# Layer 1's edge groups: two VectorE inputs placed in PSUM, the running sums scaled on ScalarE, three banks of node sums

## The chip, the cores and the metric

The kernel runs on one core of a Trainium2 chip. The metric is device time in microseconds (us), from three runs of which the median is taken. One further execution was recorded by the hardware profiler; all durations of single instructions come from that one.

## The reference, cut to what matters

A graph of 3125 nodes and 50000 edges, sorted by target, goes through two layers, each with a message-passing part, an attention-like part and a feed-forward part. The change touches the message-passing part of layer 1 alone:

```python
h_fwd = h @ W_forward.T                     # 3125 x 64
h_rev = h @ W_reverse.T
messages = h_fwd[src] * direction[:, 0:1] + h_rev[src] * direction[:, 1:2]
scores = leaky_relu(messages @ attn.T, 0.2)             # 4 heads
exp_scores = exp(scores - scores.max(axis=0))
sum_exp = segment_sum(exp_scores, dst)
norm = exp_scores / (sum_exp[dst] + 1e-10)
out = [segment_sum(messages * norm[:, h:h+1], dst) for h in range(4)]
```

For each edge a row is fetched from a table by the edge's source, combined into a message of 64 numbers and four scores, weighted by four exponentials, and summed into the edge's target node.

## The kernel before

The stages run one after the other: layer 0's mixing and feed-forward, then layer 1's sorting, mixing and feed-forward. `layer1_mix` first writes a table `tab1` of 3125 rows (forward and reverse message and scores side by side, 2 x 68 numbers). It then goes over the edges in 391 columns of 128, taken in 49 groups of 8 (`GROUP`). Node sums are kept in SBUF as `acc`, 25 tiles of 125 nodes by 4 heads by 65 numbers (64 of the message and the weight itself).

A group passes through these functions:

- `fetch`: eight indirect DMAs issued by GpSimd (L51), one for each column of 128 edges, into the tile `g1` (four buffers). They are asked for three groups ahead.
- `messages` (L1223 to L1234): VectorE combines the two halves of the fetched rows, forms the scores and their maximum over the group, and TensorE transposes the maximum.
- `maximum` (L1241 to L1247): VectorE updates the running maximum `top`, TensorE spreads it to all partitions.
- `ones_of` (L1272): for each node tile that the group's edges can reach, VectorE builds a 0/1 matrix `hot` from the edges' targets `t_dst` and the row of numbers `node`. Both inputs lie in SBUF. There are 99 of these in all, about two a group.
- `exponents` (L1252 to L1257): VectorE subtracts the maximum, ScalarE writes the exponentials into the 65th column of `v1`, and `grown`, the factor by which older sums must shrink.
- `weigh` (L1280): VectorE multiplies the messages by each head's exponential, 2048 results a partition. Both inputs lie in SBUF, the second being that 65th column.
- `products` (L1288): TensorE multiplies `hot` by `v1` into a PSUM bank `pw`, one for each node tile (four banks). One product in the code is two records in the trace.
- `add` (L1297, L1299): for a node tile that already has sums, VectorE multiplies `acc` by `grown` and then adds `pw`; a new tile is copied by ScalarE (L1302).

The loop is a software pipeline: turn i holds `messages(i)`, `weigh(i-1)`, `maximum(i)`, `products(i-1)`, `add(i-2)`, `ones_of(i)` and `exponents(i)`. TensorE, VectorE and ScalarE keep the order in which the code calls them (`manual_schedule`); GpSimd's queue holds the gathers. Twice a turn `next(todo)` puts in a piece of `galerkin`, layer 1's other part: in the first 26 turns or so two 512-wide TensorE products with their ScalarE copies and square (L1551 to L1559), VectorE's L1547 to L1563 and TensorE's L1565; later one small piece every other turn (L1602).

Of the kernel before, what the change touches and what calls it, by code (L numbers as in the profile page):

```python
# [8 lines left out]
F32 = mybir.dt.float32  # L9
I32 = mybir.dt.int32  # L10
BF16 = mybir.dt.bfloat16
AF = mybir.ActivationFunctionType
OP = mybir.AluOpType
AX = mybir.AxisListType
PSUM = bass.MemoryType.PSUM
# [4 lines left out]
P = 125  # L20
# [5 lines left out]
GROUP = 8  # L26
# [62 lines left out]
class Kernel:  # L89
# [1082 lines left out]
    def layer1_mix(self):  # L1172
        nc, tc, a = self.nc, self.tc, self.a
        W, HD = 68, 64
        with ExitStack() as m:
# [11 lines left out]
            gp = m.enter_context(tc.tile_pool(name="l1g", bufs=3))  # L1187
            ps_a = m.enter_context(tc.tile_pool(name="l1pa", bufs=2, space=PSUM))
            ps_c = m.enter_context(tc.tile_pool(name="l1pc", bufs=1, space=PSUM))
            ps_w = m.enter_context(tc.tile_pool(name="l1pw", bufs=4, space=PSUM))  # L1190
            ps_s = m.enter_context(tc.tile_pool(name="l1ps", bufs=1, space=PSUM))


# [7 lines left out]
            acc = big.tile([P, NT, 4, HD + 1], F32, name="acc1")  # L1201
# [4 lines left out]
            def tiles_of(j):  # L1206

                return max(0, (128 * j - DRIFT) // 2000), min(NT - 1, (128 * j + 127 + DRIFT) // 2000)

            begun = set()  # L1210

            def fetch(j0):
                n = min(GROUP, NJ - j0)
                g = gp.tile([128, GROUP, 2 * W], F32, name="g1", bufs=4)
                for i in range(n):
                    gather(nc, g[:, i, :], tab1[:], self.t_src[:, j0 + i:j0 + i + 1])
                return j0, n, g

            def messages(j0, n, g):

                d = self.t_dir[:, j0:j0 + n, :]
                o = gp.tile([128, GROUP, W], F32, name="msg1")
                nc.vector.tensor_mul(o[:, :n, :], g[:, :n, :W], d[:, :, 0:1].to_broadcast([128, n, W]))  # L1223
                nc.vector.tensor_mul(g[:, :n, W:], g[:, :n, W:], d[:, :, 1:2].to_broadcast([128, n, W]))
                nc.vector.tensor_add(o[:, :n, :], o[:, :n, :], g[:, :n, W:])
                s = gp.tile([128, GROUP, 4], F32, name="score1")
                nc.vector.scalar_tensor_tensor(s[:, :n, :], o[:, :n, HD:], 0.2, o[:, :n, HD:],
                                               op0=OP.mult, op1=OP.max)
                if j0 + n == NJ:
                    nc.vector.tensor_scalar(s[:, n - 1, :], s[:, n - 1, :], late, None, op0=OP.add)  # L1230
                mx = gp.tile([128, 4], F32, name="mx1")
                nc.vector.tensor_reduce(mx, s[:, :n, :].rearrange("p j h -> p h j"), AX.X, OP.max)
                pt = ps_s.tile([4, 128], F32, name="psm")
                nc.tensor.transpose(pt, mx, self.ident)  # L1234
                return o, s, pt

            def maximum(pt):

                nonlocal top
                two = gp.tile([4, 3], F32, name="top")  # L1240
                nc.vector.tensor_reduce(two[:, 2:3], pt, AX.X, OP.max)  # L1241
                nc.vector.tensor_tensor(two[:, 0:1], two[:, 2:3], top, OP.max)
                nc.vector.tensor_sub(two[:, 1:2], top, two[:, 0:1])
                top = two[:, 0:1]
                pb = ps_s.tile([128, 2, 4], F32, name="psm")
                for i in range(2):
                    nc.tensor.transpose(pb[:, i, :], two[:, i:i + 1].to_broadcast([4, 128]), self.ident[:4, :4])  # L1247
                return pb

            def exponents(n, s, pb):  # L1250
                big2 = gp.tile([128, 2, 4], F32, name="top_b", bufs=4)
                nc.vector.tensor_copy(big2, pb)  # L1252
                nc.vector.tensor_sub(s[:, :n, :], s[:, :n, :], big2[:, 0:1, :].to_broadcast([128, n, 4]))
                v = gp.tile([128, GROUP, 4, HD + 1], F32, name="v1", bufs=2)
                nc.scalar.activation(v[:, :n, :, HD], s[:, :n, :], AF.Exp)
                grown = gp.tile([128, 4], F32, name="grown", bufs=4)
                nc.scalar.activation(grown, big2[:, 1, :], AF.Exp)  # L1257
                return big2, grown, v

            def tiles_in(j0, n):  # L1260

                w0, w1 = tiles_of(j0)[0], tiles_of(j0 + n - 1)[1]
                for w in range(w0, w1 + 1):
                    js = [i for i in range(n) if tiles_of(j0 + i)[0] <= w <= tiles_of(j0 + i)[1]]
                    yield w, js[0], len(js)

            def ones_of(j0, n):

                hots = []
                for w, i0, k in tiles_in(j0, n):  # L1270
                    hot = gp.tile([128, GROUP, P], F32, name="hot", bufs=5)
                    nc.vector.scalar_tensor_tensor(  # L1272
                        hot[:, :k, :], self.t_dst[:, j0 + i0:j0 + i0 + k, None].to_broadcast([128, k, P]),
                        float(-w * P), self.node[:, None, :P].to_broadcast([128, k, P]),
                        op0=OP.add, op1=OP.is_equal)
                    hots.append(hot)
                return hots

            def weigh(n, o, v):
                nc.vector.tensor_mul(v[:, :n, :, :HD], o[:, :n, None, :HD].to_broadcast([128, n, 4, HD]),  # L1280
                                     v[:, :n, :, HD:].to_broadcast([128, n, 4, HD]))

            def products(j0, n, v, hots):
                sums = []
                for (w, i0, k), hot in zip(tiles_in(j0, n), hots):
                    pw = ps_w.tile([P, 4, HD + 1], F32, name="pw")
                    for i in range(i0, i0 + k):
                        nc.tensor.matmul(pw.rearrange("p h c -> p (h c)"), hot[:, i - i0, :],  # L1288
                                         v[:, i, :, :].rearrange("p h c -> p (h c)"),
                                         start=(i == i0), stop=(i == i0 + k - 1))  # L1290
                    sums.append(pw)
                return sums

            def add(j0, n, big2, grown, sums):
                for (w, _, _), pw in zip(tiles_in(j0, n), sums):
                    if w in begun:
                        nc.vector.tensor_mul(acc[:, w, :, :], acc[:, w, :, :],  # L1297
                                             grown[:P, :, None].to_broadcast([P, 4, HD + 1]))
                        nc.vector.tensor_add(acc[:, w, :, :], acc[:, w, :, :], pw)  # L1299
                    else:  # L1300
                        begun.add(w)
                        nc.scalar.copy(acc[:, w, :, :], pw)  # L1302
                    if j0 + n == NJ or w < tiles_of(j0 + n)[0]:
                        nc.scalar.copy(unit[:, w, :], big2[:P, 0, :])


            with tc.manual_schedule(engines={E_.PE, E_.DVE, E_.Activation}):
                todo = self.galerkin(big, wk, ps_a, ps_c, xT)
                next(todo)
                starts = [(j0, min(GROUP, NJ - j0)) for j0 in range(0, NJ, GROUP)]  # L1310
                G = len(starts)
                ahead = [fetch(starts[i][0]) for i in range(3)]
                msg, exps, summed = {}, {}, {}
                for i in range(G + 2):
                    if i + 3 < G:
                        ahead.append(fetch(starts[i + 3][0]))
                    if i < G:
                        j0, n, g = ahead[i]
                        o, s, pt = messages(j0, n, g)
                    next(todo, None)  # L1320
                    if 0 <= i - 1 < G:
                        weigh(starts[i - 1][1], msg[i - 1][0], exps[i - 1][2])
                    if i < G:
                        pb = maximum(pt)
                    if 0 <= i - 1 < G:
                        summed[i - 1] = products(*starts[i - 1], exps[i - 1][2], msg[i - 1][1])
                    if 0 <= i - 2 < G:
                        add(*starts[i - 2], *exps[i - 2][:2], summed[i - 2])
                    if i < G:
                        msg[i] = o, ones_of(j0, n)  # L1330
                        exps[i] = exponents(n, s, pb)
                    next(todo, None)
                last = exps[G - 1][0]
# [14 lines left out]
            for t0, n in CHUNKS:  # L1348
                s = slice(t0, t0 + n)
# [649 lines left out]
```

## Time and profile before

| what | value |
|---|---|
| median of three runs | 3148.76 us (3139.96 to 3158.86) |
| profiled execution, its own time | 2766.24 us |
| profiled execution, span | 2764.5 us |
| gathers of this stage, first start to last end | 1612.2 to 2190.7 us after the span's start |
| 391 gathers: busy, mean | 459.6 us, 1175 ns |
| groups 3 to 25 (start of L1223 to that of group 26) | 1665.2 to 1938.6 us |
| groups 26 to 47 | 1938.6 to 2192.8 us |

The profiled execution is 382 us shorter than the median of the runs shown. The page gives no reason for it. "Busy" is an engine's own work; "idle before" is the time that it stood still ahead of an instruction, with what ended it. A line number such as L51 can be that of a helper, so that gathers of several stages share it; they are told apart by their tiles (`g<-tab,t_src` here).

### The profile page before, as it was taken

Reading aid. Unit: us, or ns where it says so; the run is one execution under the profiler, and the core shown is the slowest. Engines: PE = TensorE matmul, PEld = TensorE weight load, DVE = VectorE, ACT = ScalarE, POOL = GpSimd, SP = SyncE. Lnnn points to the kernel's source line nnn. Section 1 sums busy time; section 2 is a strip of 40 time slices with the busy share of each in tenths; the row PEclk is TensorE's granted clock in tenths of the full one; section 3 lists DMA queues with packets and bytes.
Section 4 is the critical chain, followed back from the end, with each engine's and each line's share of the span. In section 5 each row is a group of like instructions: output and inputs, shape, how many; then the busy total and the mean of one; then the engine's idle time right before and its main releaser. Section 6 shows DMA issues by size and latency. Waiting matters only on the chain. (4 is left out here: it accounts for less than half of the span.)

```text
span 2764.5 us, 26618 instructions
## 1 busy us (share of the span) xinstructions
PE 2192.9 (79%) x9047; PEld 1649.0 (60%) x9047; DVE 1502.0 (54%) x3575; ACT 545.3 (20%) x1115; POOL 1660.4 (60%) x1486
## 2 busy tenths in 40 slices
PE   1762659999976997899999459998777756999953
PEld 1541447866754665788888336665655544666643
DVE  7986499455477901122112449998777760222226
ACT  2420000000011111222222234444000021223313
POOL 4888787774000813666666158778777507777751
PEclk9955669999986999999999669999898868999976
DMA  8930534133400303455554421111111121112252
GB/s 296 382 111 14 118 76 107 43 72 91 115 32 2 87 19 130 157 179 180 191 196 139 113 76 47 48 48 45 47 48 49 37 68 39 26 40 60 54 105 71
DMA packets 175937, 259.79 MB, mean 94 GB/s; under 512 B 53839, under 2 KB 140857, under 8 KB 172402
## 3 DMA queue, kind: packets, MB, share of 16 engines
q1 hardware_dynamic: 114273, 198.43, 23.2%
q0 software_dynamic: 52288, 47.17, 7.3%
q10 hardware_dynamic: 9222, 12.30, 1.5%
q8 instruction: 76, 1.25, 0.2%
q14 instruction: 78, 0.64, 0.1%
HBM read 173.99 MB, written 83.69 MB: 93 GB/s over the span
## 5 line engine op out<-in xcount | busy, mean ns | idle before, releaser
L58 POOL DMA_INDIRECT adj<-ch_sum,ch_place x391 | 506.3, 1295 | 150.4 <-issue 111.6
L51 POOL DMA_INDIRECT g<-tab,t_src x391 | 459.6, 1175 | 119.7 <-issue 106.8
L58 POOL DMA_INDIRECT sorted<-s_rows,pos x256 | 245.1, 958 | 183.5 <-DVE s_rows L1059 114.0
L460 PE MATMUL psum<-sup,adjT 125*125 125x256 f32 x1250 | 294.4, 395 | 51.0 <-DMA adjT<-adj 40.3
L1288 PE MATMUL pw<-v,hot 128*125 128x260 f32 x1244 | 306.9, 407 | 0.0
L51 POOL DMA_INDIRECT G<-tabg,g_src x256 | 253.7, 991 | 80.2 <-issue 71.5
L460 PEld LDWEIGHTS psum<-sup,adjT 125*125 125x125 f32 x1250 | 242.1, 195 | 92.9 <-DMA adjT<-adj 42.5
L1288 PEld LDWEIGHTS pw<-v,hot 128*125 128x125 f32 x1244 | 244.4, 200 | 43.6
L866 PE MATMUL ph<-xs,w 128*128 128x256 f32 x960 | 219.1, 387 | 23.1 <-issue 20.1
L866 PEld LDWEIGHTS ph<-xs,w 128*128 128x128 f32 x960 | 183.3, 193 | 58.0 <-issue 33.4
L894 PE MATMUL py<-w,h 128*128 128x256 f32 x960 | 216.7, 379 | 0.0
L1715 PE MATMUL fpy<-fw,fh 128*125 128x256 f32 x800 | 184.9, 387 | 33.6 <-DVE y L1717 28.3
L894 PEld LDWEIGHTS py<-w,h 128*128 128x128 f32 x960 | 180.1, 190 | 23.3
L1715 PEld LDWEIGHTS fpy<-fw,fh 128*125 128x125 f32 x800 | 151.5, 191 | 71.1 <-DVE y L1717 29.9
L868 ACT ACTIVATE h<-ph,b 128x256 f32<-128x256 f32 x240 | 113.7, 474 | 361.1 <-PE ph L866 329.3
L1707 PE MATMUL fph<-xT,fw 128*128 128x500 f32 (+1 forms) x448 | 175.5, 541 | 0.2 <-DMA fw<-in_L_ffn_W_dram 0.2
L1034 PE MATMUL pctx<-s_mv,s_ro 128*128 128x256 f32 x512 | 155.5, 415 | 1.9 <-DVE s_mv L1033 1.9
L58 POOL DMA_INDIRECT slots<-rows,abi x50 | 72.7, 1455 | 100.8 <-DVE r_cum L948 85.8
L897 DVE TENSOR_SCALAR yo<-py,own 128x256 f32<-128x256 f32 x60 | 27.8, 481 | 190.8 <-PE py L894 190.8
L1709 ACT ACTIVATE fh<-fph,cols 128x500 f32<-128x500 f32 (+1 forms) x112 | 70.3, 633 | 295.6 <-PE fph L1707 262.5
L463 DVE TENSOR_TENSOR x<-x,psum 125x512 f32<-125x512 f32 (+1 forms) x104 | 68.7, 663 | 109.6 <-PE psum L460 109.5
L1707 PEld LDWEIGHTS fph<-xT,fw 128*128 128x128 f32 x448 | 84.8, 190 | 71.4 <-issue 48.6
(537 smaller groups left out, 3352.8 us busy)
## 6 DMA issues: line engine op xcount, KB each, us to landing
adjT<-adj SPq DMA_DIRECT2D x25, 1367.2 KB
adj<-zero SPq DMA_DIRECT2D x22, 1536.0 KB
w<-in_L_ffn_W1p_dram SPq DMA_DIRECT2D x30, 1024.0 KB
w<-in_L_ffn_W2p_dram SPq DMA_DIRECT2D x30, 1024.0 KB
slots<-empty SPq DMA_DIRECT2D x1, 8448.0 KB
srow<-slots SPq DMA_DIRECT2D x30, 264.0 KB
adj<-ch_sum,ch_place POOLq DMA_INDIRECT x391
g<-tab,t_src POOLq DMA_INDIRECT x391
```

The lines of the kernel that those rows point to most:

```text
L51: nc.gpsimd.indirect_dma_start(out=out, out_offset=None, in_=table, in_offset=bass.IndirectOffsetOnAxis(ap=idx, axis=0))
L58: return nc.gpsimd.indirect_dma_start(out=table, out_offset=bass.IndirectOffsetOnAxis(ap=idx, axis=0), in_=rows, in_offset=None, **kw)
L460: nc.tensor.matmul(pm[:, i, :], mats[b][:, (a0 + i) * P:(a0 + i + 1) * P], sup[:, b, :], start=(b == b0), stop=(b == b0 + n - 1))
L463: nc.vector.tensor_add(xs, xs, pm[:, :m, :])
L866: nc.tensor.matmul(ph, w1[:, k, f * 128:(f + 1) * 128], xs[:, k, :], start=(k == 0), stop=(k == 1))
L868: nc.scalar.activation(h[:, f, :], ph, AF.Gelu, bias=b1[:, f:f + 1])
L894: nc.tensor.matmul(py, h[:, f, i * 128:(i + 1) * 128], w2[:, f, :], start=(f == 0), stop=(f == FC - 1))
L1034: nc.tensor.matmul(p1, ro[:, f - f0, :], mv, **st)
L1288: nc.tensor.matmul(pw.rearrange("p h c -> p (h c)"), hot[:, i - i0, :], v[:, i, :, :].rearrange("p h c -> p (h c)"), start=(i == i0), stop ...
L1707: nc.tensor.matmul(ph[:, :n * P], w1[:, k, f * 128:(f + 1) * 128], xT[:, k, t0 * P:(t0 + n) * P], start=(k == 0), stop=(k == 1))
L1709: nc.scalar.activation(hs[:, f, :n * P], ph[:, :n * P], AF.Gelu, bias=self.col("L1_ffn_b1", ei * FC + f))
L1715: nc.tensor.matmul(py, hs[:, f, i * P:(i + 1) * P], w2[:, f, :], start=(f == 0), stop=(f == FC - 1))
```

## The change

Three things are changed in `layer1_mix`. One PSUM bank `side` is added, and `pw` has three banks instead of four. The bank holds `number`, a copy of the first 128 numbers of `node`, which `ones_of` now reads, and `ex`, the group's exponentials, which ScalarE now writes there and copies into the 65th column of `v1`; `weigh` reads `ex`. The multiplication of `acc` by `grown` moves from VectorE to ScalarE, as four activations (one for each head, 125 x 65) with a scale held in a column, in a function `scale` of its own that is called ahead of the first `next(todo)` of the turn. `add` keeps only the addition, and is called ahead of `products`.

```diff
-            ps_w = m.enter_context(tc.tile_pool(name="l1pw", bufs=4, space=PSUM))
+            ps_w = m.enter_context(tc.tile_pool(name="l1pw", bufs=3, space=PSUM))
+            ps_e = m.enter_context(tc.tile_pool(name="l1pe", bufs=1, space=PSUM))
...
+            side = ps_e.tile([128, 512], F32, name="side")
+            ex = side[:, 0:GROUP * 4].rearrange("p (j h) -> p j h", h=4)
+            number = side[:, 128:256]
+            nc.vector.tensor_copy(number, self.node[:, :128])
...
-                nc.scalar.activation(v[:, :n, :, HD], s[:, :n, :], AF.Exp)
+                nc.scalar.activation(ex[:, :n, :], s[:, :n, :], AF.Exp)
+                nc.scalar.copy(v[:, :n, :, HD], ex[:, :n, :])
...
-                        float(-w * P), self.node[:, None, :P].to_broadcast([128, k, P]),
+                        float(-w * P), number[:, None, :P].to_broadcast([128, k, P]),
...
                 nc.vector.tensor_mul(v[:, :n, :, :HD], o[:, :n, None, :HD].to_broadcast([128, n, 4, HD]),
-                                     v[:, :n, :, HD:].to_broadcast([128, n, 4, HD]))
+                                     ex[:, :n, :, None].to_broadcast([128, n, 4, HD]))
...
-            def add(j0, n, big2, grown, sums):
+            def scale(j0, n, grown):
+
+                for w, _, _ in tiles_in(j0, n):
+                    if w in begun:
+                        for h in range(4):
+                            nc.scalar.activation(acc[:, w, h, :], acc[:, w, h, :], AF.Copy,
+                                                 scale=grown[:P, h:h + 1])
+
+            def add(j0, n, big2, sums):
                 for (w, _, _), pw in zip(tiles_in(j0, n), sums):
                     if w in begun:
-                        nc.vector.tensor_mul(acc[:, w, :, :], acc[:, w, :, :],
-                                             grown[:P, :, None].to_broadcast([P, 4, HD + 1]))
                         nc.vector.tensor_add(acc[:, w, :, :], acc[:, w, :, :], pw)
...
+                    if 0 <= i - 2 < G:
+                        scale(*starts[i - 2], exps[i - 2][1])
                     next(todo, None)
...
+                    if 0 <= i - 2 < G:
+                        add(*starts[i - 2], exps[i - 2][0], summed[i - 2])
                     if 0 <= i - 1 < G:
                         summed[i - 1] = products(*starts[i - 1], exps[i - 1][2], msg[i - 1][1])
-                    if 0 <= i - 2 < G:
-                        add(*starts[i - 2], *exps[i - 2][:2], summed[i - 2])
```

## The prediction

> **What bounds the stage now.** I read the groups of instructions in the stage's window, then the busy time by stretch, then the timeline. The groups (columns: busy us, mean ns, then idle before and what ended it):
>
> ```profile
> L51 POOL DMA_INDIRECT g<-tab,t_src x373 | 438.7, 1176 | 113.7 <-issue 101.8 <-DMA g<-tab,t_src 5.5 <-DVE hot L1272 4.0
> L1280 DVE TENSOR_TENSOR v<-msg,v 128x2048 f32<-128x2048 f32 (+1 forms) x49 | 112.0, 2287 | 0.4 <-ACT v L1255 0.4
> L1272 DVE SCALAR_TENSOR_TENSOR hot<-t_dst,node 128x1000 f32<-128x1000 f32 (+6 forms) x98 | 91.2, 972 | 0.0
> L1223 DVE TENSOR_TENSOR msg<-g,t_dir 128x544 f32<-128x544 f32 (+1 forms) x48 | 34.7, 724 | 67.8 <-DMA g<-tab,t_src 67.8
> L1299 DVE TENSOR_TENSOR acc<-acc,pw 125x260 f32<-125x260 f32 x74 | 31.5, 425 | 6.2 <-PE pw L1288 3.7
> L1297 DVE TENSOR_TENSOR acc<-acc,grown 125x260 f32<-125x260 f32 x74 | 30.7, 415 | 0.0
> ```
>
> GpSimd's idle time is nearly all "issue", 0.30 us ahead of each gather: its queue never pauses. VectorE stands still ahead of L1223 for the landing of a group's last gather, 67.8 us in all. So gathers pace the stage. By stretch (busy us of TensorE, its weight loads, VectorE, ScalarE, GpSimd; granted clock; DMA):
>
> ```profile
> 1665.20:1938.60 273.40, 249.55 (x1033) 174.41 (x1032) 248.76 (x492) 125.02 (x206) 217.61 (x184) 0.99 0.18 47
> 1938.60:2192.80 254.20, 194.54 (x762) 151.41 (x761) 195.14 (x370) 13.07 (x70) 199.42 (x174) 0.88 0.19 49
> ```
>
> In the first stretch (23 groups with galerkin work, 11.89 us each) TensorE and VectorE are both busy for 91%, close behind GpSimd. In the second (22 groups, 11.55 us each) they are busy for 77%. What makes a gather long is seen in the timeline (start, us, engine):
>
> ```profile
> 2046.71 2.30 DVE L1280 TENSOR_TENSOR v<-msg,v 128x2048 f32<-128x2048 f32 x1
> ...
> 2047.93 1.89 POOL L51 DMA_INDIRECT g<-tab,t_src  x1 [0.30 <-issue]
> ...
> 2049.94 0.43 DVE L1299 TENSOR_TENSOR acc<-acc,pw 125x260 f32<-125x260 f32 x1
> 2050.13 0.94 POOL L51 DMA_INDIRECT g<-tab,t_src  x1 [0.30 <-issue]
> ...
> 2051.08 2.04 DVE L1272 SCALAR_TENSOR_TENSOR hot<-t_dst,node 128x750 f32<-128x750 f32 x2
> 2051.38 1.45 POOL L51 DMA_INDIRECT g<-tab,t_src  x1 [0.30 <-issue]
> ```
>
> A gather that starts while L1280 runs ends 0.81 us after L1280 does; one that starts under L1299, which has one input in PSUM, takes its plain 0.94 us. Putting each of the 391 gathers beside the VectorE instruction that ran at its start, in the same timeline, gives the time above 0.945 us: 53.9 us in 47 starts under L1280, 15.3 us in 48 under L1272, 15.5 us in 45 under L1224, 5.4 us under others with two SBUF inputs, nothing in 45 under L1299, nothing under the reductions and the copy L1252. Together 90 us; with 391 x (0.944 + 0.305) = 488 us that is the 578.5 us between the first gather's start and the last one's end.
>
> **What the Trainium skill says.** "SBUF — State Buffer", section Who interferes with whom: a VectorE instruction with two SBUF inputs holds off a GpSimd instruction that reads SBUF until it ends, and one with at most one SBUF input does not. The counts above agree on both sides. "VectorE: DVE Perf Modes", The perf-mode tier table: an fp32 tensor_tensor runs at the same plain rate with a PSUM operand. L1299 (PSUM) against L1297 (SBUF) at equal size agrees, 425 against 415 ns; both are read without repetition in PSUM. "PSUM — Partial Sum Buffer", PSUM bank collisions: two engines must not touch one bank's partitions at the same time. `side` is shared by ScalarE and VectorE, but a turn's data already order them: L1272, then the subtraction, then the exponential, then `weigh`.
>
> **The change part by part.**
>
> *Inputs in PSUM.* The starts under L1280 and L1272 lose their excess: 53.9 + 15.3 = 69.2 us off GpSimd's queue. A group's eight gathers then need 8 x 1.249 = 9.99 us, plus the hit under L1224 that remains (0.345 us on average, about once a group, since L1223 starts a fixed time after the group's last gather): 10.34 us. The copy of `number` is one small instruction ahead of the groups: nothing. VectorE pays some 0.01 us for each of three instructions a group (425 against 415 ns): below 2 us over the stage, beside other work.
>
> *Scaling on ScalarE.* VectorE loses 74 instructions of 0.415 us and the gap behind each, 0.44 us from start to start: 0.66 us a group, 32 us in all. ScalarE gains 74 x 4 = 296 activations of 65 elements. Bounds: L1257 (4 elements) takes 189 ns, the scaled 125 x 125 activation `diag` 389 ns; "ScalarE: Activation LUTs", What ACT_TABLE_LOAD costs, gives an estimate of 186 + 0.833 x 65 + 93 = 333 ns. I take 0.34: 100 us busy, at most 2.7 us in a group with two scaled tiles. It needs no other activation table (the order of the changed kernel holds 78 table loads, as before). In ScalarE's order the eight stand behind the exponentials of group i-1 and ahead of the table load and the square root L1551. In the first stretch L1551 waits 88.8 us in 23 turns for VectorE, 3.9 us each; the new work (2.7 us, and 0.2 us for the copy of `ex`) fits, with 1 us or less to spare where turns also get shorter. Behind L1551 are queued the copies L1557 that free TensorE's banks, and the next exponential, which `weigh` needs some 5 us later. So I take 0; the upper end, if the spare is used up, is 0.5 us in 23 turns, 12 us. In the second stretch ScalarE is busy for 5%. The addition waits for the scaling, which stands half a turn earlier.
>
> *Copy of `ex` into `v1`.* 49 copies of 32 elements, about 0.2 us (L1304 takes 179 ns). TensorE reads the column a half turn later: 0.
>
> *Three banks.* `add` called ahead of `products` changes nothing in VectorE's or TensorE's own order. TensorE's second tile of a group now waits for the addition that frees its bank. That addition follows L1243 by 0.5 to 0.9 us; TensorE needs as long for the spreading (0.4 us) and a first tile of 2 to 8 products (0.46 us each, two records of 0.23). Cost 0; the upper end is 0.4 us for the 11 `hot` tiles of one or two columns, 4 us.
>
> *What is late next.* For each group I take the largest of its TensorE busy time, its VectorE time from L1223 to its last instruction less 0.44 us for each L1297, and GpSimd's 10.34 us. First stretch: TensorE averages 11.0 us, VectorE 11.1 - 0.66 = 10.4 us; the sum of the largest is 256.3 us against 273.4, a gain of 17.1 us. TensorE gives most of these. It waits within a turn for VectorE's maxima, so I take off 4 us: 13 us. Second stretch: GpSimd's 10.34 us is the largest in nearly all groups; 229.1 us against 254.2, a gain of 25.1 us. Groups 0 to 2 and the last additions: 2 us. Sum 40 us. From the profiled execution's 2766.24 us that gives 2726. The median of the runs is 382 us above it, for a reason that I can't see; I carry 40 us over unscaled: 3148.76 - 40 = 3108.8 us.
>
> **Rivals.**
>
> *TensorE paces more than the profile shows.* If the timed runs are long because TensorE is slower there, the first stretch is already its own. To make up 382 us, its 2192.9 us of busy time would have to be 17% longer, and more where other engines set the pace; I take 23%. Its 11.0 us become 13.5, above the 11.89 of now, and nothing is gained there; in the second stretch 8.8 us become 10.9, and 22 x (11.55 - 10.9) = 14 us remain. Against it: nothing in the profile shows a slower clock. Gain 14 to 20 us: 3132 us.
>
> *ScalarE or the banks give it back.* If the scaled activations delay L1551 and what stands behind it by over a microsecond in each of 23 turns, or TensorE waits for its bank every turn, the gain falls to 0 to 15 us: 3142 us. For it: the spare above. Against: 3.9 us of waiting.
>
> *The PSUM input does not free the port*, say because the instruction's kind counts and not its inputs. Then only VectorE's 32 us go, which end in the wait for gathers: gain 0 to 3 us. Against: 45 starts under L1299, a tensor_tensor, at 0.944 us.
>
> *Slower: repeated reading from PSUM at half rate.* `weigh` reads each exponential 64 times and `hot` repeats `number` for each column; no instruction of the trace repeats from PSUM at this size. At half rate `weigh` and two `hot` take 2.2 + 1.9 us more: VectorE needs 14.5 us in the first stretch and 13 in the second, 23 x 2.6 + 22 x 1.5 = 93 us more, 3242 us. It decides from 1.4 us in a first-stretch group (11.85 - 10.45), a rate a third worse. Against it: L1299 and L1602 read PSUM at the plain rate.
>
> **How the numbers follow.** Likeliest case (gain 25 to 60) 0.57; TensorE 0.21; given back 0.12; port not freed 0.04; half rate or another loss 0.06. A measurement of this kernel can tell about 0.5%, 16 us, from no change. All of the first case, 0.14 of the second and 0.03 of the third lie beyond it: faster 0.74, slower 0.07, the rest 0.19. The range goes from 3085 (nearly all of the 69 us) to 3150 (the third and fourth cases): about 0.87 of the chance less the tail of the first.
>
> **What would show it.** Gathers' mean falls from 1175 to about 0.99 us; none under `weigh` or `hot` above 0.95. L1280's and L1272's successors keep 2.29 and 1.19 us. The second stretch's groups take about 10.4 us, the first one's about 11.3, with TensorE over 95% busy. ScalarE's activations take about 0.34 us. I am wrong if `weigh` lasts over 3 us, if gathers still stretch under it, or if TensorE's idle ahead of the products grows.

## The result, and the profile after

The changed kernel takes 3284.22 us (median of 4 runs, 3265.11 to 3337.33) against 3148.52 us for the kernel before beside it: ratio 1.0409, interval 1.0373 to 1.0445. It is slower by 4%, where the forecast had it 40 us faster.

One thing is needed to read any number here: the same kernel before takes about 2765 us on some occasions, the quick condition (its profile above, and the runs e0 to e5), and 3120 to 3150 us on others, the long condition (the timed runs above, the profile after, and all other runs), and each kernel is compared only with the kernel before beside it.

The groups of the changed kernel's edge stage (busy us, mean ns, then idle before and what ended it; L1287 is `weigh`, L1279 `hot`, L1306 the scaling, L1247 the first instruction of `maximum`, which needs TensorE's transpose):

```profile
L51 POOL DMA_INDIRECT g<-tab,t_src x391 | 379.0, 969 | 302.6 <-DVE score L1233 188.5 <-issue 110.8 <-DVE msg L1231 2.4
L1287 DVE TENSOR_TENSOR v<-msg,side 128x2048 f32<-128x2048 f32 (+1 forms) x49 | 111.4, 2273 | 0.6 <-ACT v L1262 0.6
L1279 DVE SCALAR_TENSOR_TENSOR hot<-t_dst,side 128x1000 f32<-128x1000 f32 (+5 forms) x99 | 90.8, 953 | 0.0
L1306 ACT ACTIVATE acc<-acc,grown 125x65 f32<-125x65 f32 x296 | 75.6, 337 | 2.0 <-DVE acc L1312 2.0
L1229 DVE TENSOR_TENSOR msg<-g,t_dir 128x544 f32<-128x544 f32 (+1 forms) x49 | 35.2, 718 | 2.0 <-issue 1.3 <-DMA g<-tab,t_src 0.5
L1247 DVE TENSOR_REDUCE top<-psm 4x1 f32<-4x128 f32 x49 | 13.5, 276 | 236.7 <-remote 223.3 <-PE ln_pt L191 9.0 <-PE psm L1240 3.0
```

The first five lines are as forecast: gathers fell from 1176 to 969 ns, VectorE hardly waits for them any more (2.0 us at L1229), the PSUM inputs cost nothing, an activation takes 337 ns. The sixth is the loss: VectorE stands still for 236.7 us ahead of L1247, nearly all of it "remote", a release that the profile can't tie to the instruction that gave it. I call such a wait of over 3 us a stop. The timeline of one (start, us, engine; "issue" means that TensorE waited for nothing that is shown):

```profile
2149.81 0.94 POOL L51 DMA_INDIRECT g<-tab,t_src  x1 [0.30 <-issue]
...
2152.31 0.94 POOL L51 DMA_INDIRECT g<-tab,t_src  x1 [0.30 <-issue]
...
2152.70 0.27 PE L1240 MATMUL psm<-ident,mx 128*4 128x128 f32 x1
...
2154.77 0.59 PE L191 MATMUL ln_pt<-wkv,xT 128*125 128x512 f32 x1 [0.84 <-issue]
...
2156.20 0.59 PE L191 MATMUL ln_pt<-wkv,xT 128*125 128x512 f32 x1 [0.83 <-issue]
2156.90 0.18 PEld L191 LDWEIGHTS ln_pt<-wkv,xT 128*125 128x125 f32 x1 [1.23 <-issue]
2157.31 0.94 POOL L51 DMA_INDIRECT g<-tab,t_src  x1 [0.30 <-issue]
...
2161.37 0.28 DVE L1247 TENSOR_REDUCE top<-psm 4x1 f32<-4x128 f32 x1 [8.96 <-remote]
2161.43 0.59 ACT L1572 COPY kv<-ln_pt 125x512 f32<-125x512 f32 x1 [10.76 <-remote]
```

The transpose that L1247 waits for is recorded at 2152.70, and VectorE gets going 8.7 us later. Meanwhile TensorE issues its products some 1.4 us apart without a wait that is shown. GpSimd alone keeps its beat, a gather every 1.25 us, until it has filled its buffers at 2158.26; all is well again 3.1 us after that. In 15 of the 22 stops of over 3 us this lag is 2.6 to 3.2 us; the first has 5.9, the others less or none. The first stop is the longest, at group 2 (busy us of TensorE, its weight loads, VectorE, ScalarE, GpSimd; granted clock; DMA share, GB/s):

```profile
1900.00:1911.00 11.00, 9.93 (x39) 6.05 (x37) 10.69 (x19) 5.42 (x9) 8.42 (x9) 1.00 0.23 51
1911.00:1915.00 4.00, 0.36 (x1) 0.00 (x0) 0.24 (x1) 0.00 (x0) 3.09 (x4) 1.00 0.29 66
1915.00:1937.00 22.00, 0.00 (x0) 0.00 (x0) 0.00 (x0) 0.00 (x0) 16.51 (x19) 0.53 0.23 54
1944.00:1954.00 10.00, 9.72 (x34) 7.95 (x35) 9.16 (x18) 6.44 (x14) 3.55 (x4) 0.67 0.10 22
```

Three engines do next to nothing from 1911 to 1944 while GpSimd issues gathers. The granted clock is still 1.00 when TensorE falls idle and sinks only then, so it follows the stop; DMA engines are busy for under 30%. The packets that carry instructions (queues q8 and q14) last 1.63 us at most in this trace, and none starts between 1901 and 1953 us, so TensorE went on without one.

In this first stop it is TensorE's answer that comes late, rather than its work:

```profile
1907.66 0.27 PE L1240 MATMUL psm<-ident,mx 128*4 128x128 f32 x1 [0.74 <-DVE score L1233]
1907.77 3.59 PE L191 MATMUL ln_pt<-wkv,xT 128*125 128x512 f32 x8
...
1943.77 0.28 DVE L1247 TENSOR_REDUCE top<-psm 4x1 f32<-4x128 f32 x1 [32.52 <-remote]
1943.83 1.07 ACT L1572 COPY kv<-ln_pt 125x512 f32<-125x512 f32 x2 [34.54 <-remote]
...
1944.28 0.44 PE L1253 MATMUL psm<-ident,top 4*128 4x4 f32 x2 [32.92 <-DVE top L1248]
```

The transpose and the two products behind it are recorded as done by 1911.36, and TensorE's next instruction, L1253, waits for VectorE, which waits for the transpose. The trace also holds the times of the engines' signals (semaphore updates), which no view prints. TensorE's four outstanding ones arrive together, at 1943.71, 1943.74, 1943.80 and 1943.86 us; the last two, one for each product, are 0.06 us apart, where the recorded ends are 1.7 us apart. So the work was done long before, as far as recorded ends (which are modelled) can tell, and its signals were held back. In the quick condition (e4) each of TensorE's 298 signals in the stage comes within 0.015 us of its recorded end, and so do those of VectorE and ScalarE that are recorded here. In the stop at 2152 TensorE's own instructions come late as well, and again its last three signals arrive within 0.09 us.

After the first stop, groups last about 10 and 19.5 us by turns. From the start of group 0 to that of group 48 this stage takes 691.9 us, against 563.4 in the kernel before under the same condition (e6); what lies ahead of and behind it is alike (1886.1 and 702.9 us against 1882.5 and 703.1). So the loss, 129 of the 132 us between these two executions, is in these groups.

### The profile page after: what moved, and what is told of

It reads as the page before. It is cut to its first block, busy times and chain, and to the rows that moved or that the text cites. A ratio compares the mean times of both kernels' runs of the same rounds, so it can differ in the third digit from the quotient of the medians.

```text
span 3281.0 us, 26935 instructions
## 1 busy us (share of the span) xinstructions
PE 2298.1 (70%) x9047; PEld 1699.1 (52%) x9047; DVE 1467.3 (45%) x3502; ACT 623.6 (19%) x1460; POOL 1560.1 (48%) x1486
## 3 DMA queue, kind: packets, MB, share of 16 engines
q8 instruction: 76, 1.25, 0.2%
## 5 line engine op out<-in xcount | busy, mean ns | idle before, releaser
L58 POOL DMA_INDIRECT adj<-ch_sum,ch_place x391 | 487.9, 1248 | 147.8 <-issue 119.0
L51 POOL DMA_INDIRECT g<-tab,t_src x391 | 379.0, 969 | 302.6 <-DVE score L1233 188.5
L460 PE MATMUL psum<-sup,adjT 125*125 125x256 f32 x1250 | 328.8, 411 | 189.6 <-issue 171.1
L460 PEld LDWEIGHTS psum<-sup,adjT 125*125 125x125 f32 x1250 | 250.4, 202 | 257.3 <-issue 196.1
L1295 PE MATMUL pw<-v,hot 128*125 128x260 f32 x1244 | 338.9, 437 | 0.2 <-issue 0.2
L1295 PEld LDWEIGHTS pw<-v,hot 128*125 128x125 f32 x1244 | 266.5, 218 | 53.9 <-PE psm L1253 0.3
L1730 PE MATMUL fpy<-fw,fh 128*125 128x256 f32 x800 | 208.1, 417 | 85.1 <-DVE y L1732 35.4
L1730 PEld LDWEIGHTS fpy<-fw,fh 128*125 128x125 f32 x800 | 163.9, 208 | 135.4 <-ACT fh L1724 37.7
L1722 PE MATMUL fph<-xT,fw 128*128 128x500 f32 (+1 forms) x448 | 184.1, 559 | 38.9 <-ACT fh L1724 31.7
```

Source lines behind the costliest of these rows:

```text
L51: nc.gpsimd.indirect_dma_start(out=out, out_offset=None, in_=table, in_offset=bass.IndirectOffsetOnAxis(ap=idx, axis=0))
L58: return nc.gpsimd.indirect_dma_start(out=table, out_offset=bass.IndirectOffsetOnAxis(ap=idx, axis=0), in_=rows, in_offset=None, **kw)
L460: nc.tensor.matmul(pm[:, i, :], mats[b][:, (a0 + i) * P:(a0 + i + 1) * P], sup[:, b, :], start=(b == b0), stop=(b == b0 + n - 1))
L1722: nc.tensor.matmul(ph[:, :n * P], w1[:, k, f * 128:(f + 1) * 128], xT[:, k, t0 * P:(t0 + n) * P], start=(k == 0), stop=(k == 1))
L1730: nc.tensor.matmul(py, hs[:, f, i * P:(i + 1) * P], w2[:, f, :], start=(f == 0), stop=(f == FC - 1))
```

## Experiments in the quick condition: the parts of the change

The stage's length below is always from the start of group 0 to that of group 48.

**e0_before_again**, the kernel before, unchanged.

> The kernel before, profiled once more, because its profiled execution (2766 us) was 382 us shorter than its timed runs (3149 us). Theory A (TensorE is held: it stands still in the middle of work that waits for nothing, in dense stretches, in the timed runs of both kernels): a profile near 3150 us, with TensorE's matmuls of L460 issued about 2.8 us apart for a while as in the changed kernel's trace, late answers of TensorE after dense stretches, but in the edge groups few or none of the 9 us stops, groups still near 11.8 us. Theory B (the changed kernel brings its own waits: banks, ScalarE): the edge groups near 11.8 us and nothing late from TensorE in any stage.

Measured: 2762.0 us, stage 559.7 us (557.8 in the profile shown). The profile of before was of the quick condition.

**e1_psum_inputs_only**: the changed kernel with the multiplication back on VectorE.

```diff
-            def scale(j0, n, grown):
...
                     if w in begun:
+                        nc.vector.tensor_mul(acc[:, w, :, :], acc[:, w, :, :],
+                                             grown[:P, :, None].to_broadcast([P, 4, HD + 1]))
                         nc.vector.tensor_add(acc[:, w, :, :], acc[:, w, :, :], pw)
```

> The two PSUM inputs and the three banks, with the multiplication by grown left on VectorE. Theory A (gathers no longer hold the groups back, TensorE runs denser and is then held for some 9 us in every second group): about as slow as the changed kernel, ratio 1.03 to 1.05, gathers at 0.97 us mean, groups alternating between 10 and 19 us. Theory B (ScalarE's scaling brings the loss): 0.985 to 1.00, no alternation. My first forecast, with nothing held: 0.99.

Measured: 2693.62 us, ratio 0.975 (0.9721 to 0.978), stage 489.4 us. 82 gathers start under `weigh` and take 943 ns, 66 under `hot` and take 944.

**e2_scale_only**: the kernel before with `scale` on ScalarE and `add` moved.

```diff
-                        nc.vector.tensor_mul(acc[:, w, :, :], acc[:, w, :, :],
-                                             grown[:P, :, None].to_broadcast([P, 4, HD + 1]))
...
+                    if 0 <= i - 2 < G:
+                        scale(*starts[i - 2], exps[i - 2][1])
...
```

> Only the multiplication by grown moved to ScalarE; inputs in SBUF, four banks. Theory A: gathers still stretch under L1280 and L1272 and pace the groups, TensorE is no denser; ratio 0.99 to 1.01. Theory B (ScalarE's 296 activations are the loss): ratio 1.03 or more, with the alternation of 10 and 19 us.

Measured: 2796.09 us, ratio 1.0107 (1.0077 to 1.0138), stage 596.5 us. The multiplications had lain between `weigh` and `hot` as a gap in which a gather could start. Without them gathers fall under `hot` instead: their excess there is 45.3 us against 15.3, and 55.0 under `weigh`.

**e3_three_banks_only**: the kernel before with three banks and `add` ahead of `products`.

```diff
-            ps_w = m.enter_context(tc.tile_pool(name="l1pw", bufs=4, space=PSUM))
+            ps_w = m.enter_context(tc.tile_pool(name="l1pw", bufs=3, space=PSUM))
...
```

> Only three banks of node sums instead of four, and add called ahead of products. Theory A: ratio 0.99 to 1.01. Theory B in its other form (TensorE waits for a bank every second group, and that wait is the 9 us): ratio 1.03 or more.

Measured: 2764.25 us, ratio 0.9998 (0.9986 to 1.001). In this condition the banks cost nothing.

**e4_changed_again**, the changed kernel, unchanged.

> The changed kernel itself once more, since TensorE was held up in its first profile (stops of 9 us in every second group, matmuls of L460 2.8 us apart in a stage that the change doesn't touch), and not at all in the four profiles of e0 to e3. Theory A (the loss of 4% is TensorE being held up): where the kernel before takes about 2765 us and its profile shows no held TensorE, the changed kernel is faster than before, 2690 to 2730 us, ratio 0.973 to 0.987; where before takes about 3149 us, ratio 1.03 to 1.05 with the stops. Theory B (the two parts together bring a wait of their own, whatever TensorE does): ratio 1.03 or more in either case, groups alternating between 10 and 19 us.

Measured: 2699.31 us, ratio 0.9743 (0.9727 to 0.976), stage 487.5 us. In this condition the change gains 70 us, all of it in the stage. The same groups as above, here without any stop:

```profile
L51 POOL DMA_INDIRECT g<-tab,t_src x391 | 388.2, 993 | 119.7 <-issue 109.9 <-DMA g<-tab,t_src 4.9 <-POOL late L1197 1.0
L1229 DVE TENSOR_TENSOR msg<-g,t_dir 128x544 f32<-128x544 f32 (+1 forms) x49 | 35.3, 720 | 30.1 <-DMA g<-tab,t_src 29.5 <-issue 0.5
L1247 DVE TENSOR_REDUCE top<-psm 4x1 f32<-4x128 f32 x49 | 13.3, 272 | 4.3 <-PE psm L1240 4.3
```

And its two stretches by busy time (columns as in the forecast), answering to those of before:

```profile
1667.20:1908.00 240.80, 240.25 (x1034) 171.41 (x1033) 231.38 (x456) 163.17 (x377) 183.81 (x188) 1.00 0.21 55
1908.00:2126.10 218.10, 181.54 (x757) 142.52 (x757) 179.74 (x338) 49.47 (x229) 165.09 (x168) 0.92 0.21 54
```

**e5_changed_paced**: the changed kernel with GpSimd slowed by four memsets a group.

```diff
             def fetch(j0):
...
+                for _ in range(4):
+                    nc.gpsimd.memset(pace, 0.0)
```

> The changed kernel with four memsets of 384 elements (about 0.35 us each) put on GpSimd's queue in every group, so that eight gathers take some 11.7 us again though none is held off by VectorE. Theory A (what matters is the pace at which gathers let the groups through): ratio 0.99 to 1.01 in either case, without the 9 us stops. Theory B (the change brings waits of its own beside the gathers' pace): slower than the changed kernel by what the memsets add, ratio above 1.03.

Measured: 2783.54 us, ratio 1.0051 (1.0034 to 1.0067). The scheduler put all the memsets ahead of group 16, most of them into groups 5 to 15, which took about 17 us each, and left the rest unpaced: not the even pace that was meant, and no evidence on it.

## Experiments in the long condition: what holds TensorE's answers back

**e6_before_third, e7_paced_again, e8_psum_inputs_again**: the kernels of e0, e5 and e1 once more.

> The kernel before, profiled beside the next two. Theory A (on some chips TensorE is held when its work is packed dense; on the one of the recorded result the kernel before was held in other stages, and not in its edge groups): where this takes about 3149 us, L460's matmuls come 2.8 us apart for a while, and the edge groups still take 11.3 to 12.6 us each; where it takes about 2765 us nothing is held. Theory C (the edge groups of the kernel before are held as well, and the change only makes it worse): at about 3149 us the edge groups of before alternate too, and the stage takes over 620 us instead of 570.

> The changed kernel with GpSimd slowed by four memsets a group. Where before takes about 2765 us: ratio 1.00 to 1.01 as in e5. Where before takes about 3149 us, theory A: 0.99 to 1.02, since the groups come at the old pace and TensorE has its old pauses; theory C: 1.03 or more, since the change's other edits hold TensorE too.

> The PSUM inputs and three banks without the scaling on ScalarE. Where before takes about 2765 us: 0.97 to 0.98 as in e1. Where before takes about 3149 us, theory A: 1.02 to 1.05, since the groups come as fast as in the changed kernel; theory C in the form that ScalarE's added work is what tips it: 0.97 to 1.00.

Measured: e6 3150.69 us, stage 563.4 us, only 4 to 6 us more than in the quick condition. The line of e6 that answers to L1247 above:

```profile
L1241 DVE TENSOR_REDUCE top<-psm 4x1 f32<-4x128 f32 x49 | 13.4, 273 | 5.6 <-remote 4.0 <-PE ln_pt L191 1.1 <-PE psm L1234 0.5
```

e8 gives 3265.14 us, ratio 1.0372 (1.032 to 1.0424), stage 674.6 us: the PSUM inputs, with the three banks, bring most of the loss without the scaling. e7 gives 3302.48 us, 1.0496 (1.0452 to 1.0539): in its paced groups, 17 us each, there is no stop; the first group after them takes 49 us, and then the stops are there.

**e11_lighter_tensor**: the changed kernel with half of the contraction of galerkin's kv products left out, 1.8 us less TensorE work a group.

```diff
-                    self.token_matmul(pk, xT, t, wkv[:, :, 512 * i:512 * i + 512])
+                    self.nc.tensor.matmul(pk, xT[:, 0, t * P:(t + 1) * P], wkv[:, 0, 512 * i:512 * i + 512],
+                                          start=True, stop=True)
```

> The changed kernel with half of galerkin's products of keys and values left out (the second half of the contraction), so that TensorE has about 1.8 us less to do in each of the first 25 groups, at the changed kernel's pace of gathers. Theory A in the form that TensorE's own share of busy time tips it (some 95% borne, 100% not): at 3149 us no stops in the first 25 groups, perhaps none later, ratio below 1.00. In the form that any faster pace tips it: stops as in the changed kernel, ratio about 1.03. Where before takes about 2765 us: 0.965 to 0.975, a little under the changed kernel, as GpSimd then sets the pace at 10.3 us.

Measured: 3271.6 us (3242.26, 3246.34, 3296.85 and 3301.2) beside 3127.57, without an interval; in the profile, that of the first of these, stage 674.3 us, group 2 36.5 us, then mostly 10 and 19 us by turns. A lighter load of TensorE does not take the stops away.

**f3_scale_only_again**: e2's kernel.

> The scaling on ScalarE alone once more: gathers keep their SBUF locks. Where the kernel before takes about 2765 us, 2796 as the first time. Where it takes about 3150: if ScalarE's scaling brings the stops on, 3260 or more; if the faster groups or the PSUM inputs do, some 3180 (31 us more than before) without stops.

Measured: 3162.51 us, ratio 1.009 (1.0057 to 1.0122), stage 594.7 us: e2's loss again, and no stop. Its line for `maximum`:

```profile
L1241 DVE TENSOR_REDUCE top<-psm 4x1 f32<-4x128 f32 x49 | 13.3, 272 | 0.5 <-PE psm L1234 0.5
```

The scaling does not bring the stops on, nor does the order of `add` that comes with it. Here gathers still wait under `hot` and `weigh`, and there is one in 1.57 us on average.

**f2_one_ahead**: the changed kernel with gathers one group ahead.

```diff
-                g = gp.tile([128, GROUP, 2 * W], F32, name="g1", bufs=4)
+                g = gp.tile([128, GROUP, 2 * W], F32, name="g1", bufs=2)
...
-                ahead = [fetch(starts[i][0]) for i in range(3)]
+                ahead = [fetch(starts[i][0]) for i in range(1)]
...
-                    if i + 3 < G:
-                        ahead.append(fetch(starts[i + 3][0]))
+                    if i + 1 < G:
+                        ahead.append(fetch(starts[i + 1][0]))
```

> The changed kernel with two buffers of gathered rows instead of four, so that gathers run one group ahead and not three. If the stops feed on the backlog (a stop, then two groups in a burst, then a stop), the burst is at most one group and the stage falls from 704 us to near 575 where the kernel before takes about 3150: the kernel about 3150. If the backlog is a mere consequence, the stops stay and the kernel takes 3260 or more. Where the kernel before takes about 2765 us, gathers wait a little more and it takes 2700 to 2720.

Measured: 3283.57 us (3215.69, 3282.95, 3284.2 and 3287.24) beside 3134.48, without an interval. In the profile, that of the second of these, the stage starts some 50 us later than in the profile after (1935.8 against 1886.1), which the stage's length leaves out. Group 2 lost only 9 us, not 30: the first stop lasts as long as there are buffers to fill. But every second group stops as before (stage 658.9 us). A deep backlog is not needed.

**f1_weigh_twice**: `weigh` issued twice, so that VectorE paces the groups at 12.5 us and gathers stay free.

```diff
                         weigh(starts[i - 1][1], msg[i - 1][0], exps[i - 1][2])
+                        weigh(starts[i - 1][1], msg[i - 1][0], exps[i - 1][2])
```

> The changed kernel with `weigh` issued twice per group, writing the same values: 2.28 us more of VectorE work in every group, so that each of groups 0 to 48 takes about 12.6 us, set by VectorE itself and evenly, while every gather stays free of locks. If it is the pace of the groups that brings the stops on, they are gone where the kernel before takes about 3150 us: the edge groups take 48 x 12.6 = 605 us against 575 in the kernel before, the kernel about 3180, and gathers still run ahead but make no bursts under 12.6 us. If it is what the changed kernel adds (PSUM inputs, ScalarE's scaling), whatever the pace, groups of 20 us come back, and the kernel takes 3260 or more. Where the kernel before takes about 2765 us, both give 2699 + 48 x 2.2 = about 2800.

Measured: 3210.55 us, ratio 1.0241 (1.0192 to 1.029), stage 641.1 us. Group 2 loses 29 us. Groups 3 to 25 then take 12.3 to 13.1 us without a stop: eight gathers 1.25 us apart, then an interval of about 4 us, one gather in 1.56 us on average, with `weigh` and `hot` reading PSUM all the time. From group 29 on VectorE has less to do, groups shorten to 10.4 us, and every second one stops again. In groups 45 to 47, when no gather is left, groups of 10.4 us follow each other without a stop. So neither the PSUM reads nor the length of a group as such brings the stops on.

**f4_hot_back**: the node numbers back in SBUF, the weights still in PSUM.

```diff
-                        float(-w * P), number[:, None, :P].to_broadcast([128, k, P]),
+                        float(-w * P), self.node[:, None, :P].to_broadcast([128, k, P]),
```

> The changed kernel with the node numbers back in SBUF: only the weights lie in PSUM, so that GpSimd's gathers are locked under `hot` but not under `weigh`. Where the kernel before takes about 2765 us, most of the gain stays if the gathers then fall under `hot` seldom (2700), and half of it goes if they shift under it (2730). Where the kernel before takes about 3150: if the stops need groups near 10.3 us, this one, whose groups take 11 to 11.5, is partly or wholly free of them (3130 to 3180); if the mere PSUM input of `weigh` brings them on, 3260.

Measured: 3146.12 us, ratio 1.0041 (1.0012 to 1.007), stage 563.6 us. `hot` holds off 38 gathers (2200 ns each), which breaks their beat: after the first ten, up to 2208 us, at most eight gathers follow each other before an interval of 1.5 us or more comes (so, too, in all of e6), groups take 9.6 to 12.6 us, and nothing stops. From 2208 us on thirteen follow each other; the first stop begins 8 us later, and VectorE waits 5.2 us in group 29 and 30.1 us in group 30. It is the only place of this run that has any.

**e10_even_mild, e9_even_slow, g2_even_same**: one memset after every gather, of 8, 96 and 248 elements, with GpSimd's order fixed. Only the memset's length differs.

```diff
+            pace = big.tile([128, 96], F32, name="pace")
...
                     gather(nc, g[:, i, :], tab1[:], self.t_src[:, j0 + i:j0 + i + 1])
+                    nc.gpsimd.memset(pace, 0.0)
...
-            with tc.manual_schedule(engines={E_.PE, E_.DVE, E_.Activation}):
+            with tc.manual_schedule(engines={E_.PE, E_.DVE, E_.Activation, E_.Pool}):
```

> The same with memsets of 8 elements (about 0.1 us), groups of about 11.1 us. Theory A: where before takes about 2765 us, 0.985 to 0.995; where before takes about 3149 us it tells where the pace tips: 0.98 to 1.00 if 11.1 us is still borne, 1.03 or more with stops if not.

> The changed kernel with one memset of 96 elements (about 0.18 us) on GpSimd behind every gather, in the order of the code, so that eight gathers take about 11.8 us in every group (in e5 and e7 the memsets had all gathered in the first 16 groups). Theory A (TensorE is held once groups come faster than it can bear, whatever brings them): where before takes about 3149 us, ratio 0.99 to 1.01 with no stop of 9 us in any group; where before takes about 2765 us, 1.00 to 1.01. Theory D (reading from PSUM, ScalarE's scaling or the three banks hold TensorE at any pace): 1.03 or more at 3149 us.

> The same GpSimd time per group, spread evenly: a memset of 248 elements after every gather, so that gathers follow each other every 1.42 us and eight take about 11.4 us. If it is the missing hole that stops TensorE, not the rate of gathers, stops come back here and not in the kernel with one hole: 3200 or more. If it is the rate of gathers, both are free of stops, about 3120. Where the kernel before takes about 2765, 2750 as the other.

| run | gather to gather, median | stage | time | ratio |
|---|---|---|---|---|
| e10 | 1.26 us | 696.2 us | 3257.71 us | 1.0433 (1.0388 to 1.0477) |
| e9 | 1.30 us | 646.0 us | 3215.1 us | 1.0308 (1.0255 to 1.0361) |
| g2 | 1.44 us | 553.3 us | 3123.92 us | 0.9983 (0.9964 to 1.0002) |

The lines for `maximum`, of e10, e9 and g2 in this order:

```profile
L1249 DVE TENSOR_REDUCE top<-psm 4x1 f32<-4x128 f32 x49 | 13.5, 276 | 236.9 <-remote 223.8 <-PE ln_pt L191 8.8 <-PE psm L1242 4.2
```

```profile
L1249 DVE TENSOR_REDUCE top<-psm 4x1 f32<-4x128 f32 x49 | 13.5, 276 | 159.4 <-remote 143.8 <-PE ln_pt L191 12.4 <-PE psm L1242 1.7
```

```profile
L1249 DVE TENSOR_REDUCE top<-psm 4x1 f32<-4x128 f32 x49 | 13.4, 273 | 24.6 <-remote 17.2 <-issue 2.9 <-PE psm L1242 2.3
```

Spacing the gathers by 0.18 us more than in e10 takes 212 of 237 us of standing still away. Everything that the change brought is still in g2. (e10 and e9 ran on one occasion, g2 on another; the kernel before took 3127.57 us beside the first two and 3132.95 us beside g2.) My theory at the time was that a hole in the run of gathers lets TensorE go on; g2, which has no holes, was to stop, and did not. That theory fell.

**g1_one_hole**: nearly the same GpSimd time a group, as three memsets of 384 elements after the fourth gather.

```diff
                     gather(nc, g[:, i, :], tab1[:], self.t_src[:, j0 + i:j0 + i + 1])
+                    if i == 3:
+                        for _ in range(3):
+                            nc.gpsimd.memset(pace, 0.0)
```

> The changed kernel with a hole of about 1.4 us after every fourth gather (three memsets of 384 elements on GpSimd, its order fixed), so that eight gathers take about 8 x 1.25 + 1.4 = 11.4 us. If TensorE is stopped by gathers that follow each other every 1.25 us without a hole, and let go about 3 us after the first hole, no stop lasts and the stage takes 48 x 11.4 = 547 us against 575 in the kernel before: the kernel about 3120 where the kernel before takes 3149. If holes don't matter, stops of 9 us come back and it takes 3215 or more. Where the kernel before takes about 2765, it takes 2699 + 48 x 1.1 = 2750.

Measured: 3132.82 us, ratio 1.0007 (0.9976 to 1.0038), stage 560.3 us. Most groups take 11.6 us, but groups 16 to 19 take 83 us together, with stops of 4 to 11 us, and 35 and 37 over 14 us each. One hole a group does no better than even spacing at the same sum.

## Why the prediction was wrong

*The gathers' own step was right.* None is held off under `weigh` or `hot`; their mean is 0.97 to 0.99 us as forecast; group time where they pace is 10.3 us (e4, second stretch), the forecast's 10.34. The Trainium skill's rule in "SBUF — State Buffer", Who interferes with whom, holds here: a gather takes 943 ns with one input in PSUM (e1), 2102 ns on average under the same `weigh` with two in SBUF (f3).

*The half-rate rival and the ScalarE rival are out.* `weigh` takes 2273 ns, `hot` 953, the scaling 337 ns where 0.34 us was taken; three banks cost nothing (e3).

*The scaling's 32 us for VectorE were worth nothing.* e1 and e4 are 6 us apart beside kernels before that are 4 us apart. Alone it loses 31 us (e2): it moved the gathers' starts under `hot`. This interplay was not in the forecast.

*"What is late next", in the quick condition: right in kind, too small.* The sum gave 40 us; 70 were gained. The mis-sized term is the first stretch: 273.4 us were to become 260 (the largest of each group, less 4 us for TensorE's waits) and became 240.8, with TensorE busy for 240.25 of them. Its busy time itself fell from 249.55 us for the same number of records: a busy TensorE in the profile had included slack, so 11.0 us a group was no floor. The second stretch became 218.1 us for 229.1 forecast.

*The step that failed* is the sentence "The median of the runs is 382 us above it, for a reason that I can't see; I carry 40 us over unscaled." It took the unknown condition to be a constant added to the time. But in that condition TensorE's answers come late where GpSimd issues gathers at full beat, and that beat is what the change touches. The locks on the gathers (their being held off by VectorE), 90 us by the forecast's own count, had been slowing them to one in 1.49 us on average (e6) and so kept the answers coming. Taking 69 us of them away let the gathers run at 1.25 us, and VectorE then stood still 237 us for TensorE's answers instead of 69 us for gathers. The first rival, TensorE slower in the timed runs, came nearest, but had it slower by a fixed share, which can give no loss. No case of the forecast had a faster GpSimd hold another engine up. The forecast's profile, being of the quick condition, could not show this; the 382 us were its one sign.

*What is shown and what is not.* Shown: with everything else in place, the spacing of gathers alone turns the stops on and nearly off (e10, e9, g2); they are absent when no gather is left (f1), and absent or nearly so where locks or even memsets hold gathers to one in 1.44 us or more (e6, f3, g2). The average alone does not settle it: with one hole a group, g1 averages one in 1.48 us and still has eight stops. Not shown: what holds TensorE's signals back, and what makes the long condition. The clock, the bandwidth and the instruction packets are unlikely by the trace. In the quick condition e4 has the same 1.25 us beat and no stop, so the beat is needed but not enough. By the chips' numbers on record the condition doesn't belong to one: e0 to e3 and e9 to e11 all ran on number 4.

The nearest rival, untested, is the recording itself. The seven traces of the quick condition hold 29650 to 29690 landings of DMAs, the thirteen of the long one 10651 to 13362, though the kernels ask for the same transfers. Signals of the engines are missing too while GpSimd issues indirect DMAs: in the profile after, all 862 are there from 700 to 1050 us, where it issues none, but only 898 of 1302 in the edge stage (e4 has all of its 1304 there). So in the long condition the recorder loses events just where TensorE's signals come late. It may itself hold them back, or suffer from the same cause; g2, nearly free of stops, loses as much. No run here is known to have gone without a recording, so whether the loss is there without one is open.

The 382 us themselves lie, all but 4 to 6 of them, in stages that the change doesn't touch, and at least a part looks alike. In layer 0, GpSimd issues `adj<-ch_sum,ch_place` while TensorE works on L460. Busy time in the middle of that work, of the kernel before, in the quick condition (first) and the long one (second):

```profile
440.00:560.00 120.00, 114.12 (x535) 96.72 (x533) 79.25 (x182) 0.00 (x0) 93.44 (x86) 0.96 0.38 92
```

```profile
440.00:640.00 200.00, 45.38 (x87) 22.65 (x85) 18.91 (x57) 0.00 (x0) 151.86 (x157) 0.52 0.02 0
```

In the second GpSimd issues 157 indirect DMAs in 200 us, one in 1.27, and TensorE does 45 us of work, most of its idle time ahead of L460 being "issue"; the DMA engines are idle (0.02). In the first it works for 114 of 120 us, beside 86 issues (one in 1.40). Slowing those issues was not tried.

The best versions differ by condition: e1 and e4 in the quick one (0.975 and 0.974), and in the long one g2, which equals the kernel before (0.9983). None of them beat it in both.

## What to carry to other kernels

A lock or wait on an engine may be the brake that keeps another one going: before freeing a queue, ask what its faster beat will do to the engines that it shares nothing with on paper. When the profiled execution and the timed runs differ by 14%, a forecast from that profile is a forecast for another condition; find the stage in which the difference lies, or leave both signs open in the range. When a profile says "remote", look at when the signal came and when its work was done, and count whether the trace has all of its events. And when an operation leaves a queue, look at the gaps it filled: e2 lost 31 us because an instruction that was taken away had held a place in which gathers could start.

## What the runs showed of the hardware

In the long condition, while GpSimd issues indirect DMAs every 1.25 us, TensorE's signals reach VectorE late, mostly until some 3 us after the run of issues (33 us of waiting in group 2, about 9 us in every second group up to group 25); at 1.44 us apart there are three such waits, of 4 to 8 us. TensorE's matmuls can then start about 1.4 us apart (L191 from 2153 to 2158 us, granted clock 1.00). A multiplication of 125 x 260 (415 ns on VectorE) costs four activations of 337 ns on ScalarE. A gather that is held off ends some 0.82 us after the VectorE instruction that holds it (0.81 to 0.83 in e2, f3, f4 and g2).
